# A two-layer decoder on one core: the state space layer's instructions put in written order, its decay product moved to GpSimd, and three steps of layer 1 shifted

## The chip, the cores and the metric

The kernel runs on one core of one Trainium2 chip. The metric is the device time of one execution in microseconds (us), median of three runs. Engines are called as in the profile: PE (TensorE matmul), PEld (its weight load), DVE (VectorE), ACT (ScalarE), POOL (GpSimd), SP (SyncE, which issues the plain DMAs here).

## The reference, cut to what matters

64 sequences of 128 positions with 256 features pass through two decoder layers, all in float32. Each of the six blocks is `x = x + block(layernorm(x))`:

```python
# layer 0
zxbcdt = x @ in_proj_w.T                 # z 512, x|B|C 512+128+128, dt 8
xBC = silu(causal_depthwise_conv(xBC, 4 taps) + conv_b)
dt = softplus(dt + dt_bias); A = -exp(A_log)
for t in range(128):                     # state space scan, 8 heads of 64
    state = state * exp(A * dt_t) + (x_t * dt_t) outer B_t
    y_t = state @ C_t
y = (y + x * D) * silu(z)
y = y * rsqrt(mean(y * y) + 1e-5) * norm_w
out = y @ out_proj_w.T
# then: cross attention (16 heads) over a context of 128; a gated recurrence over the sequences
# layer 1: self attention (16 heads, 4 for keys), a wide one-head cross attention,
#          a mixture of 8 experts (2 chosen per token) with a shared expert
```

The scan is not run step by step. For one sequence and head, `y[t] = sum over s <= t of exp(sum of A*dt over (s, t]) * (C_t . B_s) * dt_s * x_s`, which is a 128x128 matrix times a matrix.

## The kernel before, in words

The work is tiled by groups `g` of G = 4 sequences (T = 512 columns), 16 groups. It runs in four stages, each with pools of its own: the state space layer (L365 to L541), cross attention and recurrence of layer 0 (`work2`), self attention, wide attention and routing of layer 1 (`work3`), and the experts (`work4`). Each piece of work is a Python generator; a `yield` ends one of its steps.

**State space stage.** `mamba_inputs(g)` normalizes a group (L366 to L382), transposes it (L389, copies L390), computes `dt` with a softplus written as a series (L427 to L445, a chain of tiny DVE operations on 128x32), and makes ten projections of 128x512: six of them (`conv`) get a bias and the last tap on ACT (L403), three taps on DVE (L407) and a SiLU as tanh on ACT and one DVE operation (`silu2`, L396 and L397); four (`gate`) get the SiLU alone. `mamba(g, b)` does one sequence: `ua` on POOL (L468); `pg` and `gm`, the product of B and C under the mask (L471, L473); `px` transposes x (L476), `xdt` multiplies by dt (L478); `seg` (L484) sums the decays by a matmul with a triangular matrix into PSUM, ACT takes the exponential in place (L488), and DVE multiplies it with `gm` into `m` (L495); `xd` is x times D on ACT (L492); `py` (L501) is eight matmuls with `m`; `y` adds `xd` on DVE (L505) and is multiplied with the gate on POOL (L506); its square sums go over ACT (L508) and POOL (L509, L511); `po` is the output projection (L516) and the sum of squares (L520), `ms` and `rs` (L525, and `power`, L182, on POOL) its inverse root, and L529 adds to x. PSUM has six banks of one kind, `mm`, and two for `seg`. `run` takes one step of each active generator a turn: `mamba_inputs(g)` starts at turn 8g and `mamba` number i at turn 2i + 9. The compiler's scheduler may still reorder each engine's instructions by its own estimates in this stage.

**Layer 1's attention stage** uses `run_units` under `manual_schedule`: there PE, DVE, ACT and POOL keep the order in which the program issues their instructions. A step yields `(units, phase)`: the generator goes on that many units later, and within a unit steps run by phase. Each group takes eight units, each holding one half (8 heads) of one sequence's attention: scores `s` (L257) with two banks of their own, minimum (L263), exponentials (L275), transposes `pt` (L287) and copies (L289, L291), `av` (L305), `pr` (L324). In between, phase 5, stand the steps of `self_inputs` (recurrence output, norm, transposes, the projections `qT` twice, `kT`, `pv`), of `wide_attention` (norm, transposes, values `pv`, `qT`, scores, transposes, `po`) and of `route`. The next stage's weights and contexts are loaded by SP; the loads of the state space stage's successor wait until the tiles whose space they take are free, the last of these for the last `po`.

Of the kernel before, what the change touches and what calls it, by code (L numbers as in the profile page):

```python
# [9 lines left out]
F32 = mybir.dt.float32  # L10
I32 = mybir.dt.int32
AF = mybir.ActivationFunctionType
ALU = mybir.AluOpType
# [4 lines left out]
P = 128  # L18
D = 256
# [22 lines left out]
def mid(ap, n):  # L42

    return ap.unsqueeze(1).to_broadcast([ap.shape[0], n, ap.shape[1]])
# [34 lines left out]
def tile_decoder(ctx: ExitStack, tc: tile.TileContext, a: dict, out: bass.AP):  # L79
# [45 lines left out]
    part = cst[:, C_PART:C_PART + 1]  # L125
    neghalf = const.tile([P, G], F32, tag="neghalf", name="neghalf")
# [47 lines left out]
    nc.gpsimd.tensor_scalar_mul(fu, fu, 0.5)  # L174
    for w in (xwq, xbq):
        nc.gpsimd.tensor_scalar_mul(w, w, -0.25)


    def power(pool, tag, src, bufs=1):

        r = pool.tile(list(src.shape), F32, tag=tag, name=tag, bufs=bufs)
        nc.gpsimd.tensor_tensor(out=r, in0=src, in1=neghalf[:, :src.shape[1]], op=ALU.pow)  # L182
        return r
# [46 lines left out]
    def project(ps, w, m0, m, rhs):  # L230

        o = ps.tile([P, T], F32, tag="mm", name="proj")
        for k in range(2):
            nc.tensor.matmul(  # L234
                o[:m, :], lhsT=w[:, k, m0:m0 + m], rhs=rhs[k], start=(k == 0), stop=(k == 1)
            )
        return o
# [125 lines left out]

    def mamba_inputs(g, work, ps, got):
        x = X[g]  # L365
        st = work.tile([P, G, 6], F32, tag="ln_st", name="ln_st", bufs=2)  # L366
        mv = work.tile([P, G, 2], F32, tag="ln_mv", name="ln_mv", bufs=2)
        for b in range(G):
            nc.vector.bn_stats(st[:, b, :], x[:, b, :])
        for b in range(G):  # L370
            nc.vector.bn_aggr(mv[:, b, :], st[:, b, :])
        ve = work.tile([P, G], F32, tag="ln_ve", name="ln_ve", bufs=2)
        nc.vector.tensor_scalar(ve, mv[:, :, 1], LN_EPS, None, ALU.add)
        rstd = power(work, "ln_rstd", ve)
        yield

        off = work.tile([P, G], F32, tag="ln_off", name="ln_off", bufs=2)
        nc.vector.scalar_tensor_tensor(off, mv[:, :, 0], -1.0, rstd, ALU.mult, ALU.mult)
        xn = work.tile([P, G, D], F32, tag="xn", name="xn")
        for b in range(G):  # L380
            nc.scalar.activation(
                xn[:, b, :], x[:, b, :], AF.Identity, bias=off[:, b:b + 1], scale=rstd[:, b:b + 1]  # L382
            )
        yield
        xnT = [work.tile([P, T], F32, tag=f"xnT{c}", name=f"xnT{c}", bufs=2) for c in range(2)]
        for c in range(2):
            pt = ps.tile([P, T], F32, tag="mm", name="pt_ln")
            for b in range(G):
                nc.tensor.transpose(pt[:, b * P:(b + 1) * P], xn[:, b, c * P:(c + 1) * P], ident)  # L389
            nc.scalar.copy(xnT[c], pt)  # L390
        yield

        def silu2(dst, u, th=None):
            if th is None:
                th = work.tile([P, T], F32, tag="th", name="th", bufs=2)
            nc.scalar.activation(th, u, AF.Tanh, scale=0.5)  # L396
            nc.vector.scalar_tensor_tensor(dst, th, 1.0, u, ALU.add, ALU.mult)  # L397

        def conv(c):
            pc = project(ps, win, 512 + c * P, P, xnT)  # L400
            acc = work.tile([P, G, P], F32, tag="acc", name="acc", bufs=2)
            pv = pc.rearrange("p (b t) -> p b t", b=G)
            nc.scalar.activation(  # L403
                acc, pv, AF.Identity, bias=convb[:, c:c + 1], scale=convw[:, c, 3:4]
            )
            for k in range(1, 4):
                nc.vector.scalar_tensor_tensor(  # L407
                    acc[:, :, k:], pv[:, :, :P - k], convw[:, c, 3 - k:4 - k], acc[:, :, k:],
                    ALU.mult, ALU.add,
                )  # L410
            silu2(xc[:, c, :], acc.rearrange("p b t -> p (b t)"), pc)

        def gate(c):
            silu2(zs[:, c, :], project(ps, win, c * P, P, xnT))

        pd = ps.tile([P, T], F32, tag="mm", name="pd")
        pdv, v, u, z, s2, dt2 = (
            pd[:, i * 32:(i + 1) * 32].rearrange("p (b h) -> p b h", b=G) for i in range(6)  # L420
        )
        for b in range(G):
            project_rows(pdv[:, b, :], xnT, win, b, slice(1280, 1288))
        r, q, dt, da = (
            work.tile([P, G, 8], F32, tag=f"dt_{i}", name=f"dt_{i}", bufs=2) for i in range(4)
        )
        nc.vector.tensor_tensor(v, pdv, mid(dtb, G), ALU.add)  # L427
        nc.scalar.activation(u, v, AF.Abs)
        nc.scalar.activation(u, u, AF.Exp, scale=-1.0)
        xc = work.tile([P, 6, T], F32, tag="xc", name="xc", bufs=2)  # L430
        conv(4)
        yield
        nc.vector.tensor_scalar(r, u, 0.5, 1.0, ALU.mult, ALU.add)
        nc.vector.reciprocal(r, r)
        nc.vector.tensor_tensor(z, u, r, ALU.mult)
        nc.scalar.activation(s2, z, AF.Square, scale=0.5)
        conv(5)
        yield
        nc.vector.tensor_scalar(q, s2, 1.0 / 17, None, ALU.mult)
        for n in (15, 13, 11, 9, 7, 5, 3):  # L440
            nc.vector.scalar_tensor_tensor(q, q, 1.0 / n, s2, ALU.add, ALU.mult)
        nc.vector.scalar_tensor_tensor(q, q, 1.0, z, ALU.add, ALU.mult)
        nc.vector.scalar_tensor_tensor(dt2, v, 0.0, q, ALU.max, ALU.add)
        nc.vector.tensor_tensor(da, dt2, mid(negA, G), ALU.mult)
        nc.vector.tensor_scalar(dt, dt2, 0.5, None, ALU.mult)  # L445
        conv(0)
        yield
        conv(1)
        conv(2)
        yield  # L450
        zs = work.tile([P, 4, T], F32, tag="zs", name="zs", bufs=2)
        gate(0)
        conv(3)
        yield
        gate(1)
        gate(2)
        gate(3)
        got[g] = xc, zs, dt, da

    def mamba(g, b, work, ps, got):  # L460
# [7 lines left out]
        nc.gpsimd.tensor_tensor(out=ua, in0=mid(upper, 8), in1=last(da[:, b, :], P), op=ALU.mult)  # L468

# [11 lines left out]
        yield  # L481
        seg = ps.tile([P, 8, P], F32, tag="seg", name="seg")
        for hf in range(2):
            nc.tensor.matmul(  # L484
                seg[:, hf * 4:hf * 4 + 4, :], lhsT=lower, rhs=ua[:, hf * 4:hf * 4 + 4, :],
                start=True, stop=True,
            )
        nc.scalar.activation(seg, seg, AF.Exp)  # L488
# [4 lines left out]
        yield  # L493
        m = work.tile([P, 8, P], F32, tag="m", name="m", bufs=2)
        nc.vector.tensor_tensor(m, seg, mid(gm, 8), ALU.mult)  # L495
        yield
        yield
# [8 lines left out]
        nc.gpsimd.tensor_tensor(out=y, in0=y, in1=zs[:, :, tb], op=ALU.mult)  # L506
        ysq = work.tile([P, 4, P], F32, tag="ysq", name="ysq")
        nc.scalar.activation(ysq, y, AF.Square)  # L508
        nc.gpsimd.tensor_tensor(out=ysq[:, 0:2], in0=ysq[:, 0:2], in1=ysq[:, 2:4], op=ALU.add)  # L509
        sq = work.tile([P, P], F32, tag="sq", name="sq", bufs=3)  # L510
        nc.gpsimd.tensor_tensor(out=sq, in0=ysq[:, 0], in1=ysq[:, 1], op=ALU.add)  # L511
        yield
        yield
# [5 lines left out]
        yield  # L519
# [6 lines left out]
        rs = power(work, "rs", ms)  # L526
        yield
        yield
# [3 lines left out]

    with phase_pool("work1", "left") as work, phase_pool("ps1", space=PSUM) as psp:
        ps = PsumPool(psp, {"mm": 6, "seg": 1})
        got = {}
        run(
            [(8 * g, mamba_inputs(g, work, ps, got)) for g in range(NG)]
            + [(2 * i + 9, mamba(i // G, i % G, work, ps, got)) for i in range(B)]
        )
# [157 lines left out]
    c2 = const.tile([P, 2, P], F32, tag="c2", name="c2", bufs=2)  # L697
    for c in range(2):
        nc.vector.tensor_scalar(c2[:, c, :], ones, inc[:, c:c + 1], 2.0, ALU.mult, ALU.mult)
    nc.vector.tensor_scalar(fb[:, 0:4], fb[:, 0:4], 0.5, None, ALU.mult)  # L700
# [35 lines left out]
    def self_inputs(g, work, ps, hc, got):  # L736
# [24 lines left out]
        for c in range(3):  # L761
            pp = project(ps, lwq if c < 2 else lwk, c * P if c < 2 else 0, P, xnT)
            dst = qT[:, c, :] if c < 2 else kT
            nc.vector.tensor_tensor(
                dst.rearrange("p (b t) -> p b t", b=G), pp.rearrange("p (b t) -> p b t", b=G),
                mid(rfT, G), ALU.mult,
            )
            if c > 0:
                yield 1, 5
# [21 lines left out]
    def wide_attention(g, work, ps):  # L791
# [13 lines left out]
        values(0)  # L805
        yield 1, 5
        xnT = transposed(work, ps, xn)
        yield 1, 5
# [25 lines left out]
        values(2)  # L834
# [7 lines left out]
        yield 2, 5  # L842
# [99 lines left out]
    with phase_pool("work3", "left") as work, phase_pool("ps3", space=PSUM) as psp:  # L942
# [40 lines left out]
        tasks += [(8 * g + ATTEND + 11, 5, cross_and_route(g, work, ps, got)) for g in range(NG)]  # L983
# [319 lines left out]
```

## Time and profile before

| | us |
|---|---|
| median of 3 runs | 3197.55 (3197.34 to 3203.16) |
| profiled execution | 3206.84 |
| its span | 3205.1 |
| PE busy | 2996.5 (93% of the span) |
| DVE busy | 1972.3 (62%) |
| ACT busy | 1861.5 (58%) |
| POOL busy | 1262.5 (39%) |
| state space stage | 0 to about 742 |
| cross attention and recurrence | about 742 to 1797 |
| layer 1's attention stage | 1797 to about 2745 |
| experts | about 2745 to the end |

Durations and idle times in the profile come from one execution, the profiled one; the runs are timed without a profile. Busy time of PE is modelled at its ends, so a matmul that is held back in the middle can look longer instead of leaving a gap. `L234` and the like are lines of the kernel before.

### The profile page before, as it was taken

To read this page: it belongs to the slowest core of one execution; us is meant where nothing else is said; L and a number is where in the kernel's file an instruction comes from. 1 tells how busy PE (TensorE), PEld (TensorE's weight loads), DVE (VectorE), ACT (ScalarE), POOL (GpSimd) and SP (SyncE) were. 2 spreads that over 40 slices of the span, in tenths; PEclk is the share of its full clock that TensorE was granted. 3 is DMA by queue.
4 is the path that set the end of the run, shared out by engine and by line. 5 is a ranking of instruction groups with operands and counts; after the bars stand their busy time and mean duration, and the time that the engine had idled before them with its cause. 6 is when DMAs were issued, how large, how long until landed. Compare 5 with 4: busy or idle time off the path is not lost.

```text
span 3205.1 us, 54587 instructions
## 1 busy us (share of the span) xinstructions
PE 2996.5 (93%) x19022; PEld 2047.4 (64%) x19022; DVE 1972.3 (62%) x4955; ACT 1861.5 (58%) x6693; POOL 1262.5 (39%) x1204
## 2 busy tenths in 40 slices
PE   7999999996999999999999699999999997899587
PEld 4565555553777777777777456666666664688354
DVE  6887887773555555555555357777878774433344
ACT  4555555553777666766776377777787873233100
POOL 3444444453434433333332222434252422333564
PEclk9999999997999999999999899999999997899888
DMA  9990000001111111111110100111111111677453
GB/s 303 342 342 31 1 1 1 1 15 42 41 32 31 40 34 31 32 39 36 29 33 21 43 14 27 59 42 60 41 60 40 54 37 59 204 222 222 129 164 120
DMA packets 192196, 246.59 MB, mean 77 GB/s; under 512 B 24624, under 2 KB 156208, under 8 KB 191920
## 3 DMA queue, kind: packets, MB, share of 16 engines
q1 hardware_dynamic: 173952, 196.92, 19.9%
q0 software_dynamic: 17968, 46.18, 4.7%
q8 instruction: 150, 2.46, 0.3%
q14 instruction: 126, 1.03, 0.1%
HBM read 113.65 MB, written 127.93 MB: 75 GB/s over the span
## 4 chain that ended last, share of the span: by engine, by line
PE 75%; ACT 8%; DVE 6%; issue 4%; POOL 2%; another core or an unknown queue 1%; DMA 1%; SPq 1%; DVEq 0%; POOLq 0%; ACTq 0%
PE proj L234 18%; PE s L257 9%; PE pt L287 6%; PE pu L664 5%; PE pu L660 5%; PE av L305 4%; ACT e L275 3%; PE po L516 3%; PE seg L484 3%; PE pv L242 2%; PE pr L324 2%; PE pgu L1112 2%; PE py L501 2%; PE pxo L242 2%; PE pd L1175 2%
## 5 line engine op out<-in xcount | busy, mean ns | idle before, releaser
L275 ACT ACTIVATE e<-s,mx 128x128 f32<-128x128 f32 x2048 | 740.3, 395 | 384.6 <-DVE mx L263 384.6
L263 DVE TENSOR_REDUCE mx<-s 128x4 f32<-128x512 f32 x512 | 331.6, 685 | 465.2 <-PE s L257 455.3
L275 ACT ACTIVATION_READ_ACCUMULATOR e<-s,mx 128x1 f32 x2048 | 476.3, 233 | 0.0
L182 POOL TENSOR_TENSOR ln_rstd<-ln_ve,neghalf 128x4 f32<-128x4 f32 x80 | 82.1, 1026 | 685.2 <-DVE ln_ve L198 555.5
L257 PE MATMUL s<-kbd,qT 64*128 64x512 f32 x1024 | 334.5, 652 | 18.5 <-POOL qT L600 8.6
L287 PEld LDWEIGHTS pt<-consts,e 128*128 128x128 f32 x2048 | 223.0, 142 | 196.5 <-issue 151.0
L234 PE MATMUL proj<-xnT,win 128*128 128x512 f32 x640 | 298.9, 611 | 16.0 <-DVE xc L397 16.0
L287 PE MATMUL pt<-consts,e 128*128 128x128 f32 x2048 | 284.1, 282 | 0.0
L660 PE MATMUL pu<-xnTb,fx 128*128 128x128 f32 x1536 | 235.6, 276 | 1.2 <-DVE xnTb L651 1.2
L664 PE MATMUL pu<-c,fu 128*128 128x128 f32 x1536 | 234.5, 275 | 1.8 <-DVE c L695 1.8
L660 PEld LDWEIGHTS pu<-xnTb,fx 128*128 128x128 f32 x1536 | 208.0, 192 | 31.3 <-issue 23.9
L234 PEld LDWEIGHTS proj<-xnT,win 128*128 128x128 f32 x640 | 119.9, 194 | 147.7 <-issue 115.0
L407 DVE SCALAR_TENSOR_TENSOR acc<-proj,convw,acc 128x508 f32<-128x508 f32 (+2 forms) x288 | 207.0, 735 | 8.3 <-ACT acc L403 7.3
L342 POOL TENSOR_TENSOR kbd<-kT,consts 128x512 f32<-128x512 f32 x192 | 202.8, 1066 | 5.3 <-PE s L257 4.7
L664 PEld LDWEIGHTS pu<-c,fu 128*128 128x128 f32 x1536 | 202.3, 192 | 2.4 <-DVE c L695 2.4
L291 DVE COPY eT<-pt 128x512 f32<-128x512 f32 x256 | 174.9, 683 | 7.4 <-PE pt L287 7.4
L305 PE MATMUL av<-eT,v 128*32 128x128 f32 x4096 | 165.8, 280 | 13.3 <-ACT eT L289 13.3
L506 POOL TENSOR_TENSOR y<-y,zs 128x512 f32<-128x512 f32 x64 | 81.4, 1271 | 230.9 <-DVE y L505 223.1
L599 POOL TENSOR_TENSOR other<-other,consts 128x512 f32<-128x512 f32 x64 | 81.4, 1272 | 198.7 <-DMA other<-raw 198.7
L1136 POOL DMA_INDIRECT ys<-ys,t_yrow x128 | 124.7, 975 | 87.9 <-DVE x L1148 38.3
L305 PEld LDWEIGHTS av<-eT,v 128*32 128x32 f32 x4096 | 96.7, 109 | 96.1 <-issue 31.4
L289 ACT COPY eT<-pt 128x512 f32<-128x512 f32 x256 | 155.6, 608 | 2.9 <-PE pt L287 2.7
(277 smaller groups left out, 6432.4 us busy)
## 6 DMA issues: line engine op xcount, KB each, us to landing
xs<-zeros SPq DMA_DIRECT2D x64, 1024.0 KB
xs<-xs SPq DMA_DIRECT2D x71, 256.0 KB
ys<-y SPq DMA_DIRECT2D x71, 256.0 KB
ctxT<-in_ctxT_dram SPq DMA_DIRECT2D x32, 512.0 KB
other<-raw SPq DMA_DIRECT2D x256, 64.0 KB
x<-in_x_dram SPq DMA_DIRECT2D x16, 512.0 KB
xo<-xo SPq DMA_DIRECT2D x64, 128.0 KB
xo<-xo SPq DMA_DIRECT2D x16, 512.0 KB
```

What stands on the lines that cost most here:

```text
L234: nc.tensor.matmul(o[:m, :], lhsT=w[:, k, m0:m0 + m], rhs=rhs[k], start=(k == 0), stop=(k == 1))
L257: nc.tensor.matmul(ss[i], lhsT=q()[rows], rhs=kb[rows, :, :], start=True, stop=True)
L263: nc.vector.tensor_reduce(mx[i], ss[i], AX.X, ALU.min)
L275: nc.scalar.activation(e[i][:, h, :], ss[i][:, h, :], AF.Exp, bias=mx[i][:, h:h + 1], scale=-1.0, accum_out=den[:, at:at + 1],)
L287: nc.tensor.transpose(pt[:, h, :], e[i][:, h, :], ident)
L289: nc.scalar.copy(eT[i], pt)
L291: nc.vector.tensor_copy(eT[i], pt)
L305: nc.tensor.matmul(av[j * 32:j * 32 + 32, c, :], lhsT=values(h), rhs=eT[h // 4][:, h % 4, :], start=(odd == 0), stop=(odd == 1),)
L342: nc.gpsimd.tensor_tensor(out=kb, in0=mid(k, 4), in1=last(mask, P), op=ALU.mult)
L407: nc.vector.scalar_tensor_tensor(acc[:, :, k:], pv[:, :, :P - k], convw[:, c, 3 - k:4 - k], acc[:, :, k:], ALU.mult, ALU.add,)
L660: nc.tensor.matmul(pu[:, i, :], lhsT=fx[:, k, m], rhs=xnT[:, k, :], start=(k == 0), stop=False)
L664: nc.tensor.matmul(pu[:, i, :], lhsT=fu[:, k, m], rhs=got["c2"][:, k, :], start=False, stop=(k == 1),)
```

## The change

The state space stage goes under `manual_schedule` with `run_units`, one sequence to a unit. `mamba_inputs` is rewritten: a helper `stage` issues at most one `conv` and one `gate` at a time; the tanh of a conv comes at the start of the stage after it, the last DVE operation of each SiLU (`finish`) is put between the next stage's taps, and the tiny steps of `dt` (`link`) are dealt out one by one between taps. `seg` is two tiles of half the size out of one pool of eight banks; ACT writes the exponential to `m` on SBUF, and POOL multiplies `m` by `gm` in place. The scaling of the weights `fu`, `xwq`, `xbq` and the making of `c2` go from the start, and from before the second stage, into units 30 and 31. In layer 1, the two `qT` projections take a unit each, the first values of the wide attention come after its transposes, the second values get a step of their own after the exponentials, and the wide attention starts a unit later.

```diff
+    def scale_weights0():
+        nc.gpsimd.tensor_scalar_mul(fu, fu, 0.5)
+        yield 1, 8
+        for w in (xwq, xbq):
+            nc.gpsimd.tensor_scalar_mul(w, w, -0.25)
+        ...
     def mamba_inputs(g, work, ps, got):
+        mv, rstd = start_norm(g, work)
+        yield (1 if g else 0), 4
+        xn = end_norm(g, work, mv, rstd, "xn")
+        yield 1, 7
         ...
-        yield
+        yield 1, 4
+        later, chain = [], []
+        def link(n=1):
+            for _ in range(min(n, len(chain))):
+                chain.pop(0)()
+        def finish():
+            if later:
+                dst, th, u = later.pop(0)
+                nc.vector.scalar_tensor_tensor(dst, th, 1.0, u, ALU.add, ALU.mult)
+                link()
+        def tanh(th, u):
+            nc.scalar.activation(th, u, AF.Tanh, scale=0.5)
+        accs = []
+        def stage(conv=None, gate=None):
+            n = len(later)
+            for acc, pc in accs:
+                tanh(pc, acc)
+            accs.clear()
+            pc = project(ps, win, 512 + conv * P, P, xnT) if conv is not None else None
+            pz = project(ps, win, gate * P, P, xnT) if gate is not None else None
+            if pc is not None:
+                acc = work.tile([P, G, P], F32, tag="acc", name="acc", bufs=2)
+                pv = pc.rearrange("p (b t) -> p b t", b=G)
+                nc.scalar.activation(
+                    acc, pv, AF.Identity, bias=convb[:, conv:conv + 1], scale=convw[:, conv, 3:4]
+                )
+            if pz is not None:
                 th = work.tile([P, T], F32, tag="th", name="th", bufs=2)
+                tanh(th, pz)
+            if n:
+                finish()
+            for k in range(1, 4 if pc is not None else 0):
                 nc.vector.scalar_tensor_tensor(
+                    acc[:, :, k:], pv[:, :, :P - k], convw[:, conv, 3 - k:4 - k], acc[:, :, k:],
                     ALU.mult, ALU.add,
                 )
+                if k == 1 and n > 1:
+                    finish()
+                else:
+                    link()
+            if n > 1 and pc is None:
+                finish()
+            if pc is not None:
+                flat = acc.rearrange("p b t -> p (b t)")
+                accs.append((flat, pc))
+                later.append((xc[:, conv, :], pc, flat))
+            if pz is not None:
+                later.append((zs[:, gate, :], th, pz))
         ...
+        stage(4)
+        yield 0, 7
+        ...
+        stage(5, 0)
+        yield 1, 4
+        link(3)
         nc.scalar.activation(s2, z, AF.Square, scale=0.5)
+        ...
+        stage(0)
+        yield 0, 7
+        stage(1, 1)
+        yield 1, 4
+        stage(2)
+        yield 0, 7
+        link(len(chain))
+        stage(3, 2)
+        yield 1, 4
+        stage(None, 3)
+        yield 0, 7
+        stage()
     def mamba(g, b, work, ps, got):
         ...
+        yield 1, 2
         ...
-        seg = ps.tile([P, 8, P], F32, tag="seg", name="seg")
+        yield 0, 5
+        m = work.tile([P, 8, P], F32, tag="m", name="m", bufs=2)
         for hf in range(2):
-            nc.tensor.matmul(
-                seg[:, hf * 4:hf * 4 + 4, :], lhsT=lower, rhs=ua[:, hf * 4:hf * 4 + 4, :],
-                start=True, stop=True,
-            )
-        nc.scalar.activation(seg, seg, AF.Exp)
+            seg = ps.tile([P, 4, P], F32, tag="mm", name="seg")
+            hs = slice(hf * 4, hf * 4 + 4)
+            nc.tensor.matmul(seg, lhsT=lower, rhs=ua[:, hs, :], start=True, stop=True)
+            nc.scalar.activation(m[:, hs, :], seg, AF.Exp)
         ...
-        m = work.tile([P, 8, P], F32, tag="m", name="m", bufs=2)
-        nc.vector.tensor_tensor(m, seg, mid(gm, 8), ALU.mult)
+        yield 1, 1
+        nc.gpsimd.tensor_tensor(out=m, in0=m, in1=mid(gm, 8), op=ALU.mult)
+        yield 0, 6
         ...
+        yield 1, 1
         ...
+        yield 1, 4.5
         ...
+        yield 0, 8
         ...
-        ps = PsumPool(psp, {"mm": 6, "seg": 1})
-        run(
-            [(8 * g, mamba_inputs(g, work, ps, got)) for g in range(NG)]
-            + [(2 * i + 9, mamba(i // G, i % G, work, ps, got)) for i in range(B)]
-        )
+    SCAN = 6
+        ps = PsumPool(psp, {"mm": 8})
+        with tc.manual_schedule(engines=PINNED):
+            run_units(
+                [(30, 8, scale_weights0())]
+                + [(max(4 * g - 1, 0), 4, mamba_inputs(g, work, ps, got)) for g in range(NG)]
+                + [(i + SCAN - 1, 3, mamba(i // G, i % G, work, ps, got)) for i in range(B)]
+            )
     def self_inputs(g, work, ps, hc, got):
-            if c > 0:
-                yield 1, 5
+            yield 1, 5
     def wide_attention(g, work, ps):
-        values(0)
         yield 1, 5
         xnT = transposed(work, ps, xn)
+        values(0)
         ...
-        values(2)
         ...
-        yield 2, 5
+        yield 1, 5
+        values(2)
+        yield 1, 5
-        tasks += [(8 * g + ATTEND + 11, 5, cross_and_route(g, work, ps, got)) for g in range(NG)]
+        tasks += [(8 * g + ATTEND + 12, 5, cross_and_route(g, work, ps, got)) for g in range(NG)]
```

## The prediction

> **What bounds the kernel now.** I read the stages first (busy time of each engine in chosen stretches; columns: stretch, its length, then PE, PEld, DVE, ACT and POOL busy with instructions, granted clock, DMA share, GB/s).
>
> ```profile
> 0.00:110.19 110.19, 89.73 (x354) 50.55 (x354) 82.84 (x217) 55.58 (x109) 43.10 (x43) 0.95 0.98 313
> 110.19:685.66 575.47, 553.66 (x2704) 336.62 (x2704) 454.31 (x975) 319.90 (x634) 263.38 (x271) 1.00 0.25 82
> 685.66:745.00 59.34, 49.78 (x270) 32.87 (x270) 34.89 (x73) 22.56 (x45) 32.20 (x40) 0.93 0.15 36
> 1890.00:2600.00 710.00, 697.91 (x5009) 447.97 (x5009) 541.91 (x1582) 551.82 (x2326) 262.06 (x225) 1.00 0.14 46
> ```
>
> The state space stage is the first three rows, layer 1's attention stage the fourth. Both are PE's. From 110.19 to 685.66 lie 13 groups of four sequences, 44.27 us each, of which PE works 553.66/13 = 42.6. No placement of the other engines can take out more than the 21.8 us that PE idles there. The first row idles 20.5, the third 9.6, so the stage has some 50 us of idle in 742. What PE idles for in the second row:
>
> ```profile
> PE proj L234 <- DVE xc L397: 12.8, 13, 1.1
> PE px L476 <- DVE y L505: 8.9, 13, 1.0
> ```
>
> Once a group a projection waits for a bank that the last half of a SiLU on DVE must free, and once the transposes of x wait for the `y` addition: 12.8 + 8.9 = 21.7, the whole idle time.
>
> In layer 1 the row shows 12.1 us of idle in 13.4 groups of 52.9 us, but more hides inside "busy" matmuls. Timeline lines (start, length) of PE and PEld, and one line of PE's waits in eight groups (2154.6 to 2577.7):
>
> ```profile
> 2200.36 1.96 PE L257 MATMUL s<-kbd,qT 64*128 64x512 f32 x4
> 2201.19 0.29 PEld L257 LDWEIGHTS s<-kbd,qT 64*128 64x128 f32 x2 [0.54 <-ACT e L275]
> 2208.48 1.13 PE L257 MATMUL s<-kbd,qT 64*128 64x512 f32 x4
> PE av L305 <- ACT eT L289: 4.3, 16, 0.3
> ```
>
> The same four score matmuls take 1.13 us, or 1.96 where their second half waits for the exponentials to leave the bank. In those eight groups the scores' row says 88.8 us for 64 sets, 1.39 each; against 1.13 that is 0.26 x 8 = 2.1 us a group, and the visible waits (4.3 + 1.6 + 1.3 over 8) are another 0.9: 3.0 us a group in which PE waits for ACT.
>
> **The state space loop, steady.** Moved, not added, on PE: every matmul stays, so its work remains 42.6 a group. DVE loses four `m` products, ACT's exponential is cut in two, and POOL gains the product, in place on SBUF. The rows (min/median/max ns):
>
> ```profile
> L495 DVE TENSOR_TENSOR m<-seg,gm x64: 1211/1221/1226, 45.6 to 727.2; 128x1024 f32<-128x1024 f32 x64
> L468 POOL TENSOR_TENSOR ua<-consts,dt x64: 1892/1898/1902, 32.9 to 715.8; 128x1024 f32<-128x1024 f32 x64
> L743 POOL TENSOR_TENSOR x<-x,xo x16: 2337/2366/2373, 1806.1 to 2542.3; 128x1024 f32<-128x1024 f32 x16
> L378 DVE SCALAR_TENSOR_TENSOR ln_off<-ln_mv,ln_rstd x16: 154/1172/1220, 9.2 to 582.2; 128x4 f32<-128x4 f32 x16
> ```
>
> DVE: 4 x 1.22 = 4.9 less, 454.31/13 = 34.9 to 30.0 a group. ACT: 4 x (2 x 0.60 - 1.01) = 0.8 more, to 25.4. POOL has no such product now; its price lies between `ua` (1.90, both inputs broadcast) and `x` in place (2.37, same size, full inputs). I take 2.37, since `m` is read in full: POOL goes from 263.38/13 = 20.3 to 29.7 a group, below PE's 42.6. So no engine's sum binds; order can.
>
> In the new order a unit (one sequence) issues on PE: pg and px 0.95, a projection 1.8, po 1.95, seg 1.9, py 1.03, then up to two projections 3.64: 11.3 us from one py to the next in three of four units, 10.5 in the fourth. The chain that must fit between them: py starts at 0; DVE `y` to 1.9; POOL `y*zs` 1.27 to 3.2; ACT's square is queued behind the gate's tanh, which waits for the projection that ends at 4.7, so it ends at 5.9; POOL's two sums 0.73 and 0.46 to 7.2; `m` 2.37 to 9.6; next py 9.6. That is 1.7 below 11.3, so `m` hides; past 4.0 us it would not. POOL's `ua` (1.90) and `rs` (0.55) fit behind `m` before the next `y*zs`. DVE is tightest in the unit with the next group's statistics: statistics 2.0, conv 2.2 and two SiLU halves stand ahead of `y`, which I put 1.9 late, still inside the chain because the square waits for the tanh anyway. Banks: with `seg` in the shared eight, I count at most seven held when a new one is asked for. So most of the two old waits should go; I leave 0.4 us a group (5.2 over 13): -16.5. Bounds: -21.7 (all), and +26 from L378: that tiny operation reads two SBUF tiles and takes 0.15 or 1.17 us, 1.17 where POOL's 128-wide products run beside it, and with `m` there it and its sister L373 (max 1.80 us in this trace) may be held 2 us a group longer in DVE's tight unit: 13 x 2. I take none of that, because both ends of the unit have slack.
>
> The Trainium skill (SBUF — State Buffer, Who interferes with whom) says why L378 stretches: a VectorE instruction with two SBUF inputs contends with a GpSimd instruction that reads SBUF, and one waits for the other in full; one with a PSUM input does not. The trace agrees (convs, one input in PSUM, stay at 639 to 748 ns with POOL at work). The rule speaks against moving `m` to GpSimd: by it alone the two small operations could each wait a whole `m`, +62 us over 13 groups on DVE; by the row, the sum above.
>
> **The start.** DVE paces it. Stages are now serial on ACT and DVE (bias 0.78, three taps 2.2, tanh 0.60, hand-offs): near 4.0 us for each of six convs from 19.8, and 2.0 of statistics, so the last x is there at 46 and PE has idled 22.5 by then (46 less 23.5 of work), then runs through. Before: 20.5, some at a lower clock. Two xwq and fu scalings (1.49 and 4.09) leave POOL's start, where they hid nothing. Net 0, bounds -6 and +8. They now stand at units 30 and 31: 4.09 against the slack of 1.7 is +2 once (0 to +4).
>
> **The tail.** After the last projection nothing fills PE, and the chain shows. Before (PE and POOL timeline):
>
> ```profile
> 721.80 1.09 PE L501 MATMUL py<-m,xdt 128*64 128x128 f32 x16
> 723.71 1.27 POOL L506 TENSOR_TENSOR y<-y,zs 128x512 f32<-128x512 f32 x1 [2.28 <-DVE y L505]
> 725.72 0.73 POOL L509 TENSOR_TENSOR ysq<-ysq 128x256 f32<-128x256 f32 x1 [0.23 <-ACT ysq L508]
> 726.52 0.46 POOL L511 TENSOR_TENSOR sq<-ysq 128x128 f32<-128x128 f32 x1
> 727.34 1.09 PE L501 MATMUL py<-m,xdt 128*64 128x128 f32 x16
> ```
>
> py follows py in 5.55 us, PE without a gap. Now `m` stands on POOL behind the sums: 726.52 is 4.72 after py; + 0.42 + 2.37 + 0.1 = 7.6 per sequence, and 8.05 where `ua` and `rs` delay the next `y*zs`. From the end of the last projection to the last py: po and seg 3.85, then 7.6 + 3 x 8.05 + 7.6 = 39.4, together 43.2; before it was 732.5 - 702.6 = 29.9. In the new order one po and half a seg more (2.8) lie behind that point, so the loss is 43.2 - 29.9 - 2.8 = +10.5, with +8 to +14 as bounds. What follows (the context load that waits for the last po) is the same.
>
> **Layer 1.** Nothing is added; three things shift by a unit. Projections and the like per unit on PE, by rows: before 4.4, 3.5, 2.0, 2.7, 4.5, 3.6, 2.0, 4.3; after 3.6, 3.5, 2.7, 2.8, 3.7, 3.6, 3.8, 3.5. ACT's extra work (normalizing 2.0, copies 0.6, exponentials) before falls as 3.5 and 3.4 in the units just ahead of the two light ones, which is where the stretched scores stand; after, the largest is 3.0 beside PE's 3.6. Summing ACT's lag unit by unit, its peaks fall from 3.0 and 1.4 us to 1.9 and 1.5. I take half of the 3.0 us away, 1.4 a group: -1.4 x 13.4 = -19; bounds -38 (nearly all) and +3. The later start of the wide attention changes order, not the length of the last group's chain.
>
> **Sum.** -16.5 + 0 + 2 + 10.5 - 19 = -23. The profiled execution took 3206.84 (span 3205.1), 9.3 above the median 3197.55; 3206.84 - 23 = 3183.8, as a median 3174.
>
> **Rivals.** Both stages lose all waits: -21.7 + 12 - 38 = -48, 3150. For it: attention in layer 0 runs 66.00 of 66.00 us in such an order; against: ACT's lag does not vanish. Chance 0.14. Only layer 1 gains: the state space stage trades its two waits for others of their size, 0 + 2 + 10.5 - 19 = -6.5, 3191. Chance 0.15. Only the state space stage gains, since the stretched scores follow ACT's sum and not its place: -4, 3193. Chance 0.10. The slower one: `m` on POOL paces the loop. If DVE's backlog makes `y` late by more than the 1.7 us, py follows py at the chain's length in every unit; a chain of 12.0 gives 48.0 a group, +3.8 x 13 = +49, with the rest +42: 3240. It decides from 11.2 us on (4 x 11.2 = 44.8, where the loss balances layer 1). For it: `m` has 1.2 us on DVE, right behind the exponential, and no square to wait for; against: my chain of 9.6. Chance 0.19. My forecast: 0.42.
>
> About 0.2% (6.4 us) is what a measurement can tell. Below 3191: the forecast, the first rival, half of the second and a third of the third, 0.67; above 3204: the fourth and a little, 0.20. The range reaches from 3140 (a little below the first rival) to 3212 (into the slow one's lower part).
>
> **What would show it.** Right: PE idle between group boundaries under 1 us a group up to the last projection; no score set of 1.96; last py some 43 us after the last projection; `m` near 2.37 on POOL. Wrong: PE waiting for POOL's `m` at py in the middle of the stage, DVE's L378 or L373 above 2 us with PE waiting behind, or groups of layer 1 still 52.9 us.

## The result, and the profile after

| | us |
|---|---|
| before, median of 22 runs | 3199.87 (3188.44 to 3207.42) |
| after, median of 22 runs | 3194.51 (3189.06 to 3204.41) |
| ratio, 95% interval | 0.999 (0.998 to 1.000) |
| profiled execution, before and after | 3206.84 and 3193.67 |

The change moved the median by -5.4 us, where -23 was forecast: less than a measurement of this kernel can tell from nothing. By stages of the two profiled executions: the state space stage ends 12.1 us earlier (first projection of the context at 748.5 and 736.4), layer 0's attention gives 3.3 more (first `lwq` projection 1819.1 and 1803.7), layer 1's stage is 4.7 **longer** (from there to the first `pgu` 940.5 and 945.2), and the experts 2.5 shorter. These sum to -13.2, more than the medians show, because the profiled execution of the kernel before lies 7 us above its median. Two stages were changed; one of them lost.

The stretches after, with the columns of those shown before (the fourth is the same 710 us of layer 1):

```profile
0.00:101.56 101.56, 80.85 (x294) 46.03 (x295) 58.17 (x141) 46.48 (x95) 37.17 (x36) 0.92 0.98 316
101.56:651.00 549.44, 547.36 (x2703) 337.94 (x2702) 394.78 (x965) 324.90 (x689) 389.38 (x329) 1.00 0.28 91
651.00:733.00 82.00, 64.85 (x333) 43.28 (x331) 37.09 (x92) 31.34 (x67) 58.47 (x55) 0.93 0.09 25
1875.00:2585.00 710.00, 691.18 (x4923) 447.07 (x4926) 563.80 (x1563) 542.91 (x2294) 254.29 (x217) 0.98 0.14 45
```

The second row is the same 13 groups: 575.47 us became 549.44, 42.26 a group, and PE idles 2.1 in all. In the third the last groups drain, with PE idle for 17 us. In the fourth PE was busy for less time (697.91 before) and issued fewer matmuls (5009 before): fewer groups fit. DVE's row is longer (541.91 before) with fewer instructions. So one DVE instruction got slower. Its row, and who waited for it (us in total, times):

```profile
L843 DVE SCALAR_TENSOR_TENSOR junk<-xn,yu x64: 413/422/5099, 1900.9 to 2687.1; 128x256 f32<-128x256 f32 x64
  ACT xn L215: 40.0, 11
```

`junk` is the wide attention's product of `xn` and `yu`, both in SBUF, whose sum goes to `qb`. Before, none of the 64 took over 427 ns. Now one in each of ten groups takes 5.1 us, and one in an eleventh 1.8. The timeline of one of the ten (start, length), DVE, POOL, ACT and PE:

```profile
2169.40 0.41 DVE L843 SCALAR_TENSOR_TENSOR junk<-xn,yu 128x256 f32<-128x256 f32 x1
2169.86 5.09 DVE L843 SCALAR_TENSOR_TENSOR junk<-xn,yu 128x256 f32<-128x256 f32 x1
2170.32 1.05 POOL L349 TENSOR_TENSOR kbd<-kT,consts 128x512 f32<-128x512 f32 x1
2171.32 2.35 POOL L766 TENSOR_TENSOR xo<-xo,hc 128x1024 f32<-128x1024 f32 x1
2173.62 1.03 POOL L349 TENSOR_TENSOR kbd<-kT,consts 128x512 f32<-128x512 f32 x1
2174.99 2.07 ACT L215 ACTIVATE xn<-x,ln_off,ln_inv 128x256 f32<-128x256 f32 x4 [3.93 <-DVE junk L843]
2175.64 0.33 PE L227 MATMUL pt_ln<-consts,xn 128*128 128x128 f32 x1 [1.55 <-ACT xn L215]
```

The slow one begins 0.46 us ahead of the first of three products that POOL runs back to back, and ends at 2174.95, 0.3 us after the last of them. A minimum waits behind it on DVE, ACT's normalization waits 3.93 us, and PE 1.55 at the transposes. In the eleventh group POOL has only one product to run there; `junk` begins 0.46 us ahead of it and again ends 0.3 us behind it:

```profile
2552.22 1.80 DVE L843 SCALAR_TENSOR_TENSOR junk<-xn,yu 128x256 f32<-128x256 f32 x1
2552.68 1.05 POOL L349 TENSOR_TENSOR kbd<-kT,consts 128x512 f32<-128x512 f32 x1
```

Before the change, the same `junk` and the same burst missed each other:

```profile
2237.96 1.04 POOL L182 TENSOR_TENSOR ln_inv<-ln_ms,neghalf 128x4 f32<-128x4 f32 x1 [1.03 <-DVE ln_ms L751]
2238.88 0.42 DVE L817 SCALAR_TENSOR_TENSOR junk<-xn,yu 128x256 f32<-128x256 f32 x1
2241.53 2.04 POOL L342 TENSOR_TENSOR kbd<-kT,consts 128x512 f32<-128x512 f32 x2
2243.53 2.35 POOL L739 TENSOR_TENSOR xo<-xo,hc 128x1024 f32<-128x1024 f32 x1
```

POOL waits in the unit before the burst for DVE's `ln_ms` (first line). Before, `junk` stood in that unit and the one ahead of it; the offset of one unit puts it into that unit and the one behind it, where POOL is free to run the burst.

In these groups PE's wait costs more than its length. Three stretches of 3 us around it:

```profile
2173.00:2176.00 3.00, 1.42 (x11) 0.99 (x9) 3.00 (x4) 1.01 (x3) 1.66 (x2) 1.00 0.00 0
2176.00:2179.00 3.00, 2.83 (x11) 2.25 (x12) 1.11 (x4) 3.00 (x13) 0.00 (x0) 0.53 0.00 0
2179.00:2182.00 3.00, 3.00 (x33) 2.62 (x32) 1.81 (x6) 2.77 (x13) 0.00 (x0) 0.90 0.02 5
```

The granted clock (third column from the end) falls to 0.53 in the 3 us behind the wait: the other seven transposes take 2.31 us in place of 0.9, and the wide scores 2.60 in place of 1.95. With 1.55 and 0.16 of waits that is 1.55 + 0.16 + 1.4 + 0.65 = 3.8 us. The clock falls to between 0.52 and 0.56 in this way in all ten groups. The length of the wait alone doesn't decide it, as the run with the offset undone shows further down.

### The profile page after: what moved, and what is told of

It is laid out like the page before. It is cut to its first block, busy times and chain, and to the rows that moved or that the text cites. A ratio compares the mean times of both kernels' runs of the same rounds, so it can differ in the third digit from the quotient of the medians.

```text
span 3191.9 us, 54612 instructions
## 1 busy us (share of the span) xinstructions
PE 2988.2 (94%) x19022; PEld 2053.1 (64%) x19022; DVE 1920.9 (60%) x4891; ACT 1864.8 (58%) x6757; POOL 1408.2 (44%) x1268
## 3 DMA queue, kind: packets, MB, share of 16 engines
q14 instruction: 128, 1.05, 0.1%
## 4 chain that ended last, share of the span: by engine, by line
PE 74%; DVE 9%; ACT 5%; POOL 4%; issue 4%; SPq 1%; DMA 1%; another core or an unknown queue 1%; DVEq 0%; POOLq 0%; ACTq 0%
PE proj L241 15%; PE s L264 7%; PE pt L294 6%; PE pu L695 5%; PE pu L691 5%; PE pgu L1139 4%; PE av L312 4%; PE pr L331 3%; PE pv L249 3%; PE po L546 2%; PE seg L519 2%; ACT e L282 2%; PE py L531 2%; PE pd L1202 2%; PE pd L1148 2%
## 5 line engine op out<-in xcount | busy, mean ns | idle before, releaser
L282 ACT ACTIVATION_READ_ACCUMULATOR e<-s,mx 128x1 f32 x2048 | 469.8, 230 | 0.0
L264 PE MATMUL s<-kbd,qT 64*128 64x512 f32 x1024 | 319.0, 648 | 14.3 <-POOL qT L631 8.4
L189 POOL TENSOR_TENSOR rn_rstd<-ln_ve,neghalf 128x1 f32<-128x1 f32 x64 | 37.2, 582 | 277.2 <-ACT prs L324 190.7
L526 POOL TENSOR_TENSOR m<-m,gm 128x1024 f32<-128x1024 f32 x64 | 151.1, 2362 | 15.3 <-ACT m L520 15.3
```

Of the source, the lines that this page charges most:

```text
L264: nc.tensor.matmul(ss[i], lhsT=q()[rows], rhs=kb[rows, :, :], start=True, stop=True)
L282: nc.scalar.activation(e[i][:, h, :], ss[i][:, h, :], AF.Exp, bias=mx[i][:, h:h + 1], scale=-1.0, accum_out=den[:, at:at + 1],)
```

## The experiments

The theory: the state space stage's gain is real, and layer 1's edits would gain too, but `junk` runs into POOL's burst. The rivals: the 12 us are scatter; layer 1's period is set by ACT's order or by PSUM banks.

The kernel before took 3138 to 3140 us beside the first two sets of runs and 3192 beside the third, so times are compared within a set only. The profiled execution of the first experiment spent 178 us behind the experts' last `pgu` where the one of before shown above spent 229, in the same code, and in layer 1's stage, which is the same code too, it spent 928.0 us where that one spent 940.5. So the end of a stage can scatter by more than a gain here, and layer 1 is compared by its steady groups. The start of the second stage repeats: the second stage starts at 736.4 us in the changed kernel and at 736.6 in the first experiment.

| kernel | ratio to before (95%) | us to before | steady group of layer 1, us |
|---|---|---|---|
| before | 1 | 0 | 52.9 |
| after | 0.999 (0.998 to 1.000) | -5 | 54.6 |
| state space stage alone | 0.9965 (0.9951 to 0.9979) | -10 | 52.9 |
| layer 1 alone | 1.0027 (1.0016 to 1.0039) | +9 | 54.7 |
| junk from PSUM | 0.9911 (0.9897 to 0.9924) | -27 | 51.7 |
| junk a unit earlier | 0.9860 (0.9845 to 0.9875) | -45 | 50.5 |
| offset undone | 1.0063 (1.0051 to 1.0075) | +19 | 54.9 |
| junk earlier, queries joined | 0.9911 (0.9897 to 0.9925) | -28 | 51.7 |
| junk earlier, values as before | 0.9945 (0.9929 to 0.9962) | -16 | 52.1 |
| half of xo + hc | 0.9888 (0.9867 to 0.9909) | -34 | 51.7 |
| m on VectorE, from PSUM | 1.0137 (1.0122 to 1.0151) | +44 | (state space stage +50) |
| m on VectorE, from SBUF | 1.0051 (1.0034 to 1.0067) | +16 | (state space stage +18) |
| last six m on VectorE | 0.9930 (0.9916 to 0.9945) | -20 | (state space stage -15) |
| both cures | 0.9808 (0.9790 to 0.9825) | -59 | 50.5 |

A group's time is the distance between the starts of two groups' wide scores, in mid-stage. The notes on the state space stage are against after.

### The two halves apart

The first kernel takes back the four edits of layer 1 (the last of them is shown), the second makes only them:

```diff
-        tasks += [(8 * g + ATTEND + 12, 5, cross_and_route(...)) ...]
+        tasks += [(8 * g + ATTEND + 11, 5, cross_and_route(...)) ...]
```

> Only the state space stage is changed; layer 1 is as before. Theory (the state space stage gained about 12 us, and layer 1's edits gave about as much back): the time is 12 to 16 us under the kernel before, layer 1's groups run at 52.9 us as before, and no junk instruction of VectorE is longer than 0.43 us. Rival (the 12 us of the trace are the scatter of one execution): within 6 us of the kernel before.

> Only layer 1's edits on the kernel before. Theory (the shifted junk meets GpSimd's burst of kbd, xo+hc, kbd): one junk of each group takes about 5 us, the groups run at 54.6 us, and the time is 2 to 9 us above the kernel before. Rival (the long junk is a consequence of the state space stage's new place in time or memory): junk stays at 0.42 us, groups run at 50 to 51 us, and the time is 20 to 45 us under the kernel before.

The state space stage alone gains 10 us and has no `junk` over 427 ns. Layer 1 alone loses 9 us, with `junk` up to 5078 ns: the collision needs nothing of the state space stage. The first gain is 2 us short of the theory's 12 to 16, the second number lies in its range, and both rivals fall.

### What holds junk

First its operand, with the order of all engines unchanged:

```diff
-                    junk, xn[:, b, :], 1.0, yu[:, :D], ALU.mult, ALU.mult, ...
+                    junk, pp[:, :D], 1.0, yu[:, :D], ALU.mult, ALU.mult, ...
```

> The changed kernel, with junk's first operand read from the projection in PSUM instead of xn in SBUF, so that the instruction has one SBUF operand (the shift qb that it sums is then another number; exp's argument goes through qb only by an addition that is subtracted again). The order on all engines is the same. Theory (two SBUF operands beside GpSimd): every junk takes 0.4 to 0.5 us, the groups run at 50 to 51 us, and the time is 35 to 50 us under the changed kernel. Rival (the groups are at 54.6 us because of ScalarE's order or the PSUM banks, and the long junk only stands in a gap): junk is short, and the time is within 8 us of the changed kernel. Second rival (any VectorE instruction at this place is held): junk stays at 5 us.

```profile
L843 DVE SCALAR_TENSOR_TENSOR junk<-proj,yu x64: 423/424/425, 1904.7 to 2655.8; 128x256 f32<-128x256 f32 x64
  ACT qT L841: 102.0, 32
```

With one SBUF operand none of the 64 takes over 425 ns, though most pairs of the second projection still start 0.36 us into the burst's last product, and one runs from its `kbd` into its `xo`. The gain, 27 us against before and 22 against after, is less than forecast. The edit brought a wait of its own, which may be why: DVE now stands 102 us in 32 waits for ACT's `qT`, which reads the same bank (second line). So the operand is shown to be what matters; the size had to come from the next run, which moves `junk` instead (`shifts` issues the `junk` instructions of the sequences named):

```diff
         xnT = transposed(work, ps, xn)
         values(0)
+        shifts((0, 1))
         yield 1, 5
         ...
-            for b in range(2 * c, 2 * c + 2): ...
+            if c == 0:
+                shifts((2, 3))
```

> The changed kernel, with the four junk instructions of a group one unit earlier: two behind values(0), two in the first projection's unit, the units of group time in which the kernel before had them. The sums are the same. Theory: no junk over 0.6 us, groups at 50 to 51 us, time 35 to 50 us under the changed kernel. Rival (ScalarE's order or the PSUM banks set the 54.6 us): within 8 us of the changed kernel. Second rival (GpSimd's burst moves with VectorE, and another instruction with two SBUF operands is caught instead): another VectorE group shows a maximum of some us and the groups stay over 53 us.

45 us under before, 40 under after (by the two ratios to before), groups at 50.5: the theory's numbers. Last, the other partner. Here GpSimd's sum is shortened and DVE's order left alone:

```diff
-        nc.gpsimd.tensor_tensor(out=xo, in0=xo, in1=mid(hc, G), op=ALU.add)
+        nc.gpsimd.tensor_tensor(out=xo[:, :2], in0=xo[:, :2], in1=mid(hc, 2), op=ALU.add)
```

> The changed kernel with GpSimd's sum xo + hc over two of the four sequences only (the other two are left without hc, so the numbers after it differ). GpSimd's burst kbd, xo+hc, kbd then is shorter by the half of 2.35 us, about 1.1 us; VectorE's order is untouched. Theory (the long junk ends when the burst ends): its maximum falls from 5.1 to 3.9 to 4.1 us, and the groups by 0.5 to 1.2 us. Rival (junk is held by something else of fixed length, a transfer or a read by another engine): the maximum stays at 5.0 us or more.

The long `junk` falls to 3.0 us, more than forecast. The timeline says why:

```profile
2154.31 3.01 DVE L843 SCALAR_TENSOR_TENSOR junk<-xn,yu 128x256 f32<-128x256 f32 x1
2154.75 1.05 POOL L349 TENSOR_TENSOR kbd<-kT,consts 128x512 f32<-128x512 f32 x1
2155.75 1.27 POOL L766 TENSOR_TENSOR xo<-xo,hc 128x512 f32<-128x512 f32 x1
2157.71 1.04 POOL L349 TENSOR_TENSOR kbd<-kT,consts 128x512 f32<-128x512 f32 x1 [0.69 <-PE s L264]
```

The sum ends at 2157.02, the last `kbd` is not ready, POOL pauses for 0.69 us, and `junk` ends at 2157.32, again 0.3 us behind the end of POOL's unbroken run. So with one, two and three products in the run `junk` takes 1.80, 3.01 and 5.09 us and ends 0.3 us behind the pause. By the records it starts first, and in 0.42 us it would be over just ahead of the first product's record; what holds it from there no run shows. 1.1 us of the 2.1 come from the shorter sum and 1.0 from the `kbd` that no longer follows at once. PE then waits 3.3 us in 20 times and its clock stays at 1.00, so 2.1 us less of `junk` give 2.9 us a group.

The Trainium skill (SBUF — State Buffer, Who interferes with whom) states this conflict: a VectorE instruction with two SBUF inputs contends with a GpSimd instruction that reads SBUF, the port pair that they share is an exclusive lock, and issue order decides who blocks. These runs agree on the operands (424 ns against 5.1 us). They add the length of the wait, three GpSimd instructions in a row, and by the records it is the instruction that started first that waits.

### Which edit of layer 1 brings the gain

```diff
-        tasks += [(8 * g + ATTEND + 12, 5, cross_and_route(...)) ...]
+        tasks += [(8 * g + ATTEND + 11, 5, cross_and_route(...)) ...]
```

> The changed kernel with the wide attention's start at ATTEND + 11 again; the three edits of layer 1's units stay. Junk is then in the units that the kernel before had. Theory (the offset alone carries the harm): no junk over 0.6 us, groups at 49 to 51 us, time 30 to 45 us under the kernel before, like the run with junk a unit earlier. Rival (the offset is what makes the evened units gain, because one unit earlier the wide attention waits for its group's self-attention): junk is short, and groups stay at 51.5 us or more, time 8 to 15 us under the kernel before.

The theory failed here: `junk` is short (at most 872 ns), and yet the kernel is 19 us slower than before, worse than the rival's number too. PE's waits from 1930 to 2600 us, the place in PE's timeline, DVE and POOL there, and two stretches of 3 us:

```profile
PE pv L249 <- DVE xnT L231: 25.1, 12, 2.5
2214.75 1.39 PE L249 MATMUL pv<-lwv,xnT 128*128 128x64 f32 x11
2215.98 1.04 PE L227 MATMUL pt_ln<-consts,xn 128*128 128x128 f32 x8
2219.16 2.00 PE L249 MATMUL pv<-ywv,ctxT 128*128 128x256 f32 x8 [2.14 <-DVE xnT L231]
2216.33 2.17 DVE L212 SCALAR_TENSOR_TENSOR ln_off<-ln_mv,ln_rstd 128x4 f32<-128x4 f32 x1
2218.43 0.68 DVE L231 COPY xnT<-pt_ln 128x512 f32<-128x512 f32 x1
2216.12 2.36 POOL L770 TENSOR_TENSOR x<-x,xo 128x1024 f32<-128x1024 f32 x1
2216.00:2219.00 3.00, 1.02 (x10) 0.78 (x8) 3.00 (x3) 3.00 (x16) 2.81 (x3) 1.00 0.12 44
2219.00:2222.00 3.00, 2.84 (x16) 2.25 (x20) 0.80 (x2) 2.34 (x5) 2.63 (x3) 1.00 0.80 225
```

One unit earlier the self-attention's `pv`, the two transposes and the first values ask for four banks in a row, and that pool has three; PE waits 2.1 us for DVE's copy `xnT`. The copy is late because the conflict has found another instruction: `ln_off`, ahead of the copy on DVE, has two SBUF operands, takes 2.17 us (0.16 in the median) and ends together with POOL's sum `x`. In all 12 groups PE's wait is `ln_off`'s time less 0.03 us, from 1.02 beside 1.05 to 2.50 beside 2.53. So short `junk` instructions did not mean that the conflict was gone. That the offset is needed by the values' new place rests on the wait's releaser and the order; no run isolates it from `ln_off`, and the wait is half of the 4.4 us by which a group is longer than with `junk` a unit earlier. The clock stays at 1.00 behind this wait (last line), and behind seven more of the 11 of at least 2.1 us; behind three it fell to 0.5.

Two more took one edit back in the kernel with `junk` earlier, the queries' split and the values' places:

```diff
-            yield 1, 5
+            if c > 0:
+                yield 1, 5
```

> The kernel with junk a unit earlier, with the first two query projections of the self-attention in one unit again as in the kernel before; the values' places and the offset stay. It tells which of layer 1's edits brings the 34 us that the stage gains once junk is out of the way. If the split of the queries brings it: groups at 50.5 to 52 us, 20 to 40 us above the kernel with junk a unit earlier. If the values' places bring it: within 10 us of that kernel.

```diff
+        values(0)
         yield 1, 5
         xnT = transposed(work, ps, xn)
-        values(0)
         ...
+        values(2)
         e = work.tile([P, G, P], F32, tag="e2", name="e2")
         ...
-        yield 1, 5
-        values(2)
-        yield 1, 5
+        yield 2, 5
```

> The kernel with junk a unit earlier, with the wide attention's values at their old places (the first pair a unit ahead of the transposes, the second in the unit of the exps); the split of the queries and the offset stay. Joining the queries cost 19 us there. Theory (the edits share the gain of 34 us by the PSUM banks that they free in crowded units): 8 to 20 us above the kernel with junk a unit earlier. Rival (the queries' split alone brings the gain and the values' places nothing): within 5 us of it. Second rival (the values must be apart because of the offset): over 25 us above it.

Joined queries cost 1.2 us a group (the ratios differ by 0.0051, 16 us, which lies between the two forecasts), the old places of the values 1.6 (0.0085, 27 us, of which 13 such groups explain 21). PE's largest wait in each, 1930 to 2600 us:

```profile
PE pr L331 <- DVE oT L327: 16.3, 13, 1.3
PE av L312 <- ACT eT L296: 14.2, 14, 1.8
```

So both edits are needed, and together they cost more than the 2.4 a group that layer 1's edits bring. The largest waits are different ones, for a result of DVE with the queries joined and of ACT with the values back; that the edits act through PSUM banks is not shown. The 27 us lie in the second rival's range (over 25), but the intervals of the two ratios reach down to 17, into the theory's; its reason, the offset, stays open. A third share is possible: before, two small instructions with two SBUF operands are held beside POOL in most groups, `ln_off` for up to 1534 ns and `ln_inv` with a median of 995; with `junk` a unit earlier `ln_inv` takes 98. No run isolates what that is worth.

### What m on GpSimd is worth

```diff
+        on_dve, segs = True, []
         ...
-            nc.scalar.activation(m[:, hs, :], seg, AF.Exp)
+            segs.append(seg)
+            nc.scalar.activation(seg if on_dve else m[:, hs, :], seg, AF.Exp)
         ...
-        nc.gpsimd.tensor_tensor(out=m, in0=m, in1=mid(gm, 8), op=ALU.mult)
+        if on_dve:
+            for hf in range(2):
+                hs = slice(hf * 4, hf * 4 + 4)
+                nc.vector.tensor_tensor(m[:, hs, :], segs[hf], mid(gm, 4), ALU.mult)
         ...
```

> The changed kernel with the decays' exp left in the two halves in PSUM and multiplied by VectorE from there, in all 64 sequences (as before the change), in the new unit order. Theory (the new order takes the waits away and the engine of the product matters only in the tail): the 13 steady groups stay at 42 to 43 us each, the tail from the last projection to the last py falls from 43 to 30 to 35 us, and the first projection of the second stage comes 8 to 13 us earlier than in the changed kernel. Rival (VectorE at 72% of the stage has no room for 64 products of 1.2 to 1.4 us in a row, 5 us of each group): groups go to 43.5 us or more, PE waits for VectorE in the steady loop, and the stage ends no earlier or up to 20 us later.

> The changed kernel with the product m on VectorE in all sequences, but from the copy in SBUF, so that the PSUM banks come free as in the changed kernel. With the exps left in PSUM the stage was 50 us longer, and PE waited for the bank that x's update frees. Theory (the banks held longer were the cost, VectorE has room: 72% busy plus 64 products): groups at 42.5 to 44 us, the stage within 15 us of the changed kernel's, the tail 8 us shorter. Rival (VectorE's own load was the cost): groups at 45 us or more, the stage 35 us or more longer. Second rival (two SBUF operands beside a GpSimd that is busy most of the time): m of 1.2 us takes over 2 us in the mean, and the stage is over 60 us longer.

The diff belongs to the first; the second changes only the engine, `nc.vector` for `nc.gpsimd`. From the start of the last projection's last matmul to that of the last `py` matmul the changed kernel takes 45.1 us (676.9 to 722.0). In the first kernel that projection comes 65 us later (742.2), and the drain takes 30.3. Its groups take 46.9 us and the stage is 50 longer: the rival's direction, 30 us past its bound. PE waits (150 to 650 us) for DVE's update of x, which frees `po`'s bank, so this part of the cost comes by way of a bank. In the second kernel the projection comes 33 us later (709.8), the drain takes 31.6, the groups take 44.6, and the stage is 18 longer: both just past the theory's bounds, and short of both rivals. The wait of the first, a PE wait of the second in the same stretch, the product in the first and in the second (min/median/max ns), and one long product of the second beside POOL:

```profile
PE proj L241 <- DVE x L564: 29.3, 22, 2.3
PE py L531 <- DVE m L526: 16.7, 11, 1.5
L531 DVE TENSOR_TENSOR m<-seg,gm x128: 673/679/681, 63.4 to 771.4; 128x512 f32<-128x512 f32 x128
L526 DVE TENSOR_TENSOR m<-m,gm x64: 1215/1480/2644, 64.4 to 738.4; 128x1024 f32<-128x1024 f32 x64
266.00 2.63 DVE L526 TENSOR_TENSOR m<-m,gm 128x1024 f32<-128x1024 f32 x1
265.66 1.90 POOL L500 TENSOR_TENSOR ua<-consts,dt 128x1024 f32<-128x1024 f32 x1
```

With two SBUF operands `m` takes up to 2.6 us where 1.2 is the least, and all 13 such products start 0.34 us behind POOL's `ua`; halves read from PSUM never stretch. It is the same contention, in the stage where it was looked for. It holds POOL too: `sq` takes up to 1332 ns in the second kernel and 464 at most in the changed one. So in this order the move to GpSimd gains 33 us before the drain and loses 14 in it, where nothing covers the 2.36 us. The cure is to leave the last sequences on VectorE, with the rest as in the first of the two:

```diff
+        on_dve, segs = g * G + b >= B - 6, []
         ...
```

> The changed kernel with the product on VectorE, from PSUM, in the last six sequences alone. Theory (in the tail GpSimd's sum per sequence, 7.2 us of m, ua, rs, y, ysq, sq, sets the pace): the last projection to the last py takes 30 to 35 us in place of 43, the steady groups stay at 42.3 us, and the second stage starts 8 to 13 us earlier. Rival (the chain from seg over exp, m, py and po sets the pace whatever engine multiplies): under 4 us.

The drain takes 30.3 us (677.5 to 707.8) in place of 45.1, and the second stage starts at 721.4, 15.0 earlier, above the 8 to 13 forecast. Both cures in one kernel:

> Both cures together on the changed kernel: junk a unit earlier, and the product on VectorE from PSUM in the last six sequences. Each alone stood at 45 us and at 20 us under the kernel before on this kind of run (the second with the long junk still in it, so 15 us by itself). Theory (two separate stages, so the gains add): 55 to 65 us under the kernel before, second stage from 731 us, layer 1's groups at 49 us. Rival (what one stage saves is waited for at the next one's transfers): 45 to 50 us under.

59 us under before, a ratio 0.018 below the changed kernel's: the gains add. The second stage starts at 722.5, earlier than the 731 forecast, and the groups take 50.5 and not 49.

## Why the prediction was wrong, point by point

**Steady state space loop: right way, too small.** -16.5 forecast, -26.0 measured (575.47 to 549.44), which is beyond the bound of -21.7 that was called all. Both old waits vanished; the 0.4 us a group that was kept back did not appear, and PE's busy time, taken as fixed at 42.6, fell to 42.1. The rows of its matmuls don't show why (the projections take 602 ns in the mean in both kernels). The +26 for L378 and L373 did not come: `ln_off` takes 152/491/1303 ns (min/median/max) in this stage, shorter than before in the middle, and `ln_ve` at most 249. In the steady part PE waits for `m` once, 0.8 us.

**`m` on POOL and the drain: right.** The product took 2362 ns (2.37 forecast), last projection to last `py` 43.0 us (43.2), so the loss is 43.0 - 29.9 - 2.8 = 10.3 (10.5). PE and POOL at its end:

```profile
710.45 2.34 POOL L526 TENSOR_TENSOR m<-m,gm 128x1024 f32<-128x1024 f32 x1
712.84 1.09 PE L531 MATMUL py<-m,xdt 128*64 128x128 f32 x16 [1.12 <-POOL m L526]
718.05 2.34 POOL L526 TENSOR_TENSOR m<-m,gm 128x1024 f32<-128x1024 f32 x1
720.45 1.97 PE L531 MATMUL py<-m,xdt 128*64 128x128 f32 x16 [4.47 <-POOL m L526]
```

**Start and scalings:** what is left of the stage's -12.1 is +3.6, against 0 + 2 and within their bounds.

**Layer 1: the step that failed.** -19 was worked out from ACT's lag alone ("Nothing is added; three things shift by a unit"). The lag did shrink: in the 110 us from 2150, before has two score sets of 1.96 and one near 1.55 a group, after has one of 1.96 and one of 1.31; that one of 1.96 stayed, with `junk` a unit earlier too, also contradicts "no score set of 1.96". Without the collision the edits are worth 2.4 us a group (52.9 to 50.5) against 1.4 forecast. What the step left out is the move of `junk` past POOL's queue; it put the wait that this brings at nothing. Its price is 54.6 - 50.5 = 4.1 us in each of ten groups and 51.2 - 50.5 = 0.7 in the eleventh, 42 us in all; the runs with and without it differ by 40. The conflict was named in the prediction, with its rule, but only for the stage where GpSimd got new work; in layer 1 neither engine got any, and only their order changed.

**The rivals.** "Only the state space stage gains" gave 3193, and 3194.5 came out, but not for its reason: the stretched scores did follow their place, and their gain was eaten by another wait. That the number came out is luck. "Only layer 1 gains" gave 3191, nearly the same number, and has the stages the wrong way round. `m` pacing the loop did not happen.

## What to carry to other kernels

When steps move by a unit, look at every VectorE instruction with two SBUF operands among them and at what GpSimd runs in its new unit: the pair can cost ten times the instruction's length with no work added. When one instruction is out of the way, look again, since the next step can bring another into it. Read the granted clock behind a PE wait of over a microsecond: the matmuls there may run at half of it, or not. A product that hides in a full loop shows in the drain, so let the last tiles use the faster engine.

## What was not expected of the hardware

- A VectorE instruction of 0.42 us with two SBUF operands waited through three GpSimd instructions in a row, 5.1 us, and ended 0.3 us after GpSimd's first pause; behind one and two instructions it took 1.8 and 3.0 us.
- After a PE wait of 1.55 us the granted clock was 0.53 for the next 3 us, and much the same in all ten such groups. After 13 waits of 1.26 us (queries joined) and eight of 2.1 us (offset undone) it stayed at 1.00; what decides between them is not shown. The Trainium skill (TensorE: Matmul & The Clock Gate, What's actually happening) puts the drop behind at least one idle window of about 3.4 us; here PE was busy for 1.42 of the 3 us ahead of the fall.
